# Two transformer layers on one core: the short tile moved to the front, one tile left behind the last batch, and four smaller moves

## The chip, the cores and the metric

The program runs on one core of a Trainium2 chip. The metric is the device time of one execution in microseconds, the median of the runs; lower is better. TensorE is called PE here (PEld is its weight load), VectorE DVE, ScalarE ACT, GpSimd POOL and SyncE SP.

## The reference

The input `x` has 8 batches of 100 rows of 512 values, so 800 rows. A context of 8 times 722 rows of 512 values goes beside it. Two layers follow each other, and every step is added to `x`:

```
x = x + attention0(layernorm(x), context)        # 16 heads of 32, causal
x = x + experts0(layernorm(x))                   # 8 experts, width 2048, the 2 best per row, gelu
x = x + attention1(layernorm(x), context)        # 16 heads of 64, keys and values: the
                                                 # normalised rows and a projection of the context
x = x + experts1(layernorm(x))                   # 8 experts, width 1024, the 2 best per row, silu gate
```

`experts1` ends in a norm of its own: the two answers of a row are weighted and added, the sum is normalised, multiplied by `ln_gamma`, and shifted by `ln_beta`, before it goes onto `x`. All values are float32. A layernorm needs mean and variance of each row and the reciprocal root of the variance.

## The kernel before

The 800 rows stand in SBUF as seven tiles of up to 128 partitions (`rows`, L71): six of 128 rows and a last one, tile 6, of 32. The program is written with a framework that sets all semaphores and also plans the order of the instructions on each engine: it takes what is ready by its own cost model, with the place in the program as priority, so an instruction can stand well ahead of, or behind, the place where it is written.

**Norms.** `moments` (L126) makes mean and variance on DVE (two instructions), `factors` (L134) the reciprocal root: ACT takes the root (L139, L141), DVE the reciprocal (L142) and the shift (L144). ACT holds one set of function tables at a time; the root and the exponential of the softmax are in different ones, and a load of a table shows as `ACT_TABLE_LOAD`.

**Layer 0.** After attention 0, a loop over the seven tiles (L629) projects the output, normalises it, and computes router logits one tile behind (`logits0`). When the last tile of a group is there (`GROUPS[0]`: tiles 0 to 2, 3 to 4, 5 to 6), `Route.group` (L238) picks the two best experts of each row on DVE, ranks the rows of each expert with two pairs of matmuls (L259, L260), and POOL sends each tile twice by an indirect DMA to its place in the DRAM table `sent` (L274). `Route.order` (L281) then sorts the experts by load and reads their order into registers of SP and POOL, after which SP may load the first weights of the experts.

**Experts.** `work_off` (L386) goes over eight jobs. `arrived` (L345) fetches a job's rows from `sent` and turns them on PE; `hidden0` or `hidden1` and `products` are the matmuls; `returned` (L375) writes the answers to DRAM. `midway`, where it is given, is called at the fifth job (k = 4), behind the fetch for the sixth. In layer 0 it fetches a context.

**Attention 1.** 64 units, one for each batch `b` and pair of heads `ic`, in that order. A unit computes keys and values of the context (L432, L444; 13 units read them from DRAM, where they were left earlier), the scores (L793), the softmax (L797 to L804) and, one unit later, the turned weights (`turned`, L815) and the weighted sum (`attended`, L832). The softmax's reciprocal sums must be spread over the partitions of the result. For the first three batches they are widened on POOL (L807) and turned on PE (L837). For the other batches SP writes them to DRAM and reads them back as a broadcast `over` (L810, L812), and DVE multiplies later (L850).

The seven output tiles follow as their batches end: `due` (L910 to L914) puts `output` (projection by 16 matmul passes L891, add, norm) of a tile two units behind the batch that ends it, `logits1` one unit on, and the group's routing one further. The outputs of tiles 0 to 4 come at units 18, 26, 34, 50 and 58; tiles 5 and 6 both end behind the last batch, at the end of the loop (L935). `GROUPS[1]` is (0 to 1), (2 to 3), (4), (5 to 6).

**Experts 1 and the last norm.** `gain` and `bias` are fetched on ACT's queue ahead of the jobs (L944, L946). Behind the jobs POOL gathers two answers per row and tile (`fetch`, L340), DVE weights and adds them into `acc` (L1003, L1005), normalises, multiplies by `gain`, adds to `x`, and SP writes the tile out (L1015). The add of `bias` to `x` (L1011, on POOL) is written in that last loop.

Of the kernel before, what the change touches and what calls it, by code (L numbers as in the profile page):

```python
# [13 lines left out]
P = 128  # L14
D = 512
# [22 lines left out]
ROWS = NE * NT  # L38
GROUPS = ((0, 3), (3, 5), (5, NTILE)), ((0, 2), (2, 4), (4, 5), (5, NTILE))
LAST = NT - NT // P * P  # L40

# [25 lines left out]
def two_layers(ctx: ExitStack, tc: tile.TileContext, a: dict, out: bass.AP):  # L67
    nc = tc.nc
    x_in = a["x"].rearrange("b t d -> (b t) d")
    y_out = out.rearrange("b t d -> (b t) d")  # L70
    rows = [min(P, NT - i * P) for i in range(NTILE)]  # L71

# [30 lines left out]
    x = const.tile([P, NTILE, D], F32, name="x")  # L103
    nc.vector.memset(x[:, NTILE - 1, :], 0.0)
    for i0, i1 in ((0, 1), (1, 3), (3, NTILE - 1)):
        nc.scalar.dma_start(out=x[:, i0:i1, :], in_=x_in[i0 * P : i1 * P].rearrange("(i p) d -> p i d", p=P))
    nc.scalar.dma_start(out=x[:LAST, NTILE - 1, :], in_=x_in[NT - LAST :])

# [6 lines left out]
    eps2 = const.tile([P, 1], F32, name="eps2")  # L115
    nc.vector.memset(eps2, EPS * EPS)
    rank = const.tile([P, NE], F32, name="rank")
    for e in range(NE):
# [14 lines left out]

    def factors(mv, tag, twice=False):  # L134


        r = small.tile([P, 1], F32, tag=f"r{tag}", name=f"r{tag}")
        if twice:
            nc.scalar.activation(r, mv[:, 1:], AF.Sqrt, bias=eps2, scale=1.0 + EPS)  # L139
        else:  # L140
            nc.scalar.activation(r, mv[:, 1:], AF.Sqrt, bias=eps)  # L141
        nc.vector.reciprocal(r, r)  # L142
        t = small.tile([P, 1], F32, tag=f"t{tag}", name=f"t{tag}")
        nc.vector.scalar_tensor_tensor(t, mv[:, :1], -1.0, r, ALU.mult, ALU.mult)  # L144
        return r, t
# [61 lines left out]
    class Route:  # L207


        def __init__(self, layer, psum, tag):  # L210
# [7 lines left out]
            self.sel = routes.tile([P, NTILE, NE], F32, tag="sel", name=f"sel{layer}")  # L218
            nc.vector.memset(self.sel[:, NTILE - 1, :], 0.0)
            self.before = routes.tile([P, NTILE + 1, NE], F32, tag="before", name=f"before{layer}")  # L220
# [17 lines left out]
        def group(self, i0, i1, xn, held=()):  # L238
# [6 lines left out]
            at2 = self.largest(other, self.m[1][:, i0:i1], 2)  # L245
            full = g if i1 < NTILE else g - 1
            if full:
                nc.vector.tensor_tensor(self.sel[:, i0 : i0 + full, :], at1[:, :full], at2[:, :full], ALU.add)
            if full < g:
                nc.vector.tensor_tensor(self.sel[:LAST, i1 - 1, :], at1[:LAST, full], at2[:LAST, full], ALU.add)  # L250
            for i in range(i0, i1):
# [225 lines left out]
    with tc.tile_pool(name="a0", bufs=1) as ap, tc.tile_pool(name="a0w", bufs=3) as aw, tc.tile_pool(  # L477
# [92 lines left out]
        for i in range(NTILE):  # L570
            xn = aw.tile([P, D], F32, tag="xn", name="xn0")
            scaled(xn, x[:, i, :], *factors(moments(x[:, i, :], "a0"), "a"))
            to_columns(xT, xn, i * P, rows[i], ps)
            nc.gpsimd.tensor_tensor(x[:, i, :], x[:, i, :], o_b, ALU.add)
# [46 lines left out]
        def logits0(i):  # L621
            xT = xTf[:, :, i * P : i * P + rows[i]]
            to_columns(xT, xl[:, i, :], 0, rows[i], ps)
            router_logits(route.logits, i, xT, wg0, bg0, ps, "av")
            for i0, i1 in GROUPS[0]:
                if i1 == i + 1:
                    route.group(i0, i1, lambda i: xl[:, i, :], late if i1 == NTILE else ())

        for i in range(NTILE):  # L629
            w, t0 = rows[i], i * P  # L630
            if i % 4 == 0:
# [42 lines left out]
    with f0, tc.tile_pool(name="f0w", bufs=2) as fw, tc.tile_pool(  # L674
# [57 lines left out]
        for i in range(NTILE):  # L732
# [9 lines left out]
            scaled(xn, x[:, i, :], *factors(moments(x[:, i, :], "a1"), "b", twice=True))  # L742
            to_columns(xT1, xn, i * P, rows[i], ps, gamma1, beta1)
            nc.gpsimd.tensor_tensor(x[:, i, :], x[:, i, :], bo, ALU.add)
# [4 lines left out]
    with tc.tile_pool(name="a1", bufs=1) as ap, ExitStack() as later, tc.tile_pool(  # L749
# [25 lines left out]
        def values(b, ic, mT):  # L775
# [5 lines left out]
            return mv  # L781

        def weighed(b, ic, kT, mT):

# [19 lines left out]
            nc.vector.reciprocal(sums, sums)  # L804
            if b < len(EARLY):
                over = aw.tile([T, 2, H1], F32, tag="share", name="wide1", bufs=4)
                nc.gpsimd.tensor_copy(over, sums.unsqueeze(2).to_broadcast([T, 2, H1]))  # L807
                return prs, over
# [23 lines left out]
        def attended(b, ic, v, mv, prT, over):  # L832


            po = ps.tile([P, 2, T], F32, tag="tp", name="ps_av1")
            if b < len(EARLY):
                nc.tensor.transpose(po[:, 1, :], over.rearrange("t j d -> t (j d)"), ident[:T, :T])  # L837
# [6 lines left out]
            mine = qT[:, ic, b * T : (b + 1) * T]  # L844
            if b < len(EARLY):
                wide = small.tile([P, T], F32, tag="over", name="over2")
                nc.scalar.copy(wide, po[:, 1, :])
                return nc.vector.tensor_tensor(mine, po[:, 0, :], wide, ALU.mult)
# [37 lines left out]
        def output(i):  # L886

            w, t0 = rows[i], i * P
            po = ps.tile([P, D], F32, tag="tp", name="ps_o1")
# [5 lines left out]
            xn = sends[i] = aw.tile([P, D], F32, tag="xn", name="xnf1")  # L895
            scaled(xn, x[:, i, :], *factors(moments(x[:, i, :], "f1"), "a"))

# [5 lines left out]
        def sent_on(i):  # L903

            for i0, i1 in GROUPS[1]:
                if i1 == i + 1:
                    route.group(i0, i1, lambda i: sends[i])
# [3 lines left out]
        for i in range(NTILE):  # L911
            n = min(t0 + T for t0 in range(0, NT, T) if t0 + T >= i * P + rows[i]) // T * IC + 2
            for k, step in enumerate((output, logits1, sent_on)):
# [19 lines left out]
        divide()  # L933
        attended(*before[:4], *turned(*before[4]))()
        for step, i in due[len(units)]:  # L935
# [4 lines left out]
    with tc.tile_pool(name="f1", bufs=1) as fp, tc.tile_pool(name="f1w", bufs=2) as fw, tc.tile_pool(  # L940
        name="f1p", bufs=2, space=bass.MemoryType.PSUM
    ) as ps:
        gain = fp.tile([P, D], F32, name="gain")
        nc.scalar.dma_start(out=gain, in_=a["ln_gamma"].partition_broadcast(P))  # L944
        bias = fp.tile([P, D], F32, name="bias")
        nc.scalar.dma_start(out=bias, in_=a["ln_beta"].partition_broadcast(P))  # L946
        where, more, (m1, m2) = route.where, route.more, route.m
# [27 lines left out]

        def work1(jobs, first=None):
            work_off(
                jobs, lambda e, r0, n: arrived(1, e, r0, n, fw, ps), hidden1,
                lambda e, n, h, wd: products(n, h, [wd(g) for g in range(NF // 4)], NF, fw, ps),
                lambda e, r0, n, yT: returned(1, e, r0, n, yT, fw, ps), first,  # L980
            )
# [6 lines left out]
            for e in range(NE)  # L988
        ], W_L1F)
        rest(  # L990
# [3 lines left out]

        acc = fp.tile([P, NTILE, D], F32, name="acc")
        nc.vector.memset(acc[:, NTILE - 1, :], 0.0)
        for i in range(NTILE):
# [11 lines left out]
        for i in range(NTILE):  # L1009
            w = rows[i]  # L1010
            nc.gpsimd.tensor_tensor(x[:, i, :], x[:, i, :], bias, ALU.add)  # L1011
            scaled(acc[:, i, :], acc[:, i, :], *factors(moments(acc[:, i, :], "out"), "a"))
            nc.vector.tensor_tensor(acc[:, i, :], acc[:, i, :], gain, ALU.mult)  # L1013
            nc.vector.tensor_tensor(x[:, i, :], x[:, i, :], acc[:, i, :], ALU.add)  # L1014
            nc.sync.dma_start(out=y_out[i * P : i * P + w], in_=x[:w, i, :])  # L1015

# [69 lines left out]
```

## Time and profile before

| | |
|---|---|
| median of 3 runs | 1872.75 us (1872.5 to 1874.85) |
| the profiled execution | 1873.61 us, span 1872.1 us |
| mean granted PE clock | 0.962 |
| PE busy | 1730.2 us, 92% of the span |
| DVE, ACT, POOL busy | 593.0, 482.6, 151.6 us |
| attention 0 and its outputs | to about 232 us |
| experts 0 | 247 to 636 us |
| attention 1, last unit's weights turned | 1474 us |
| first expert matmul of layer 1 | 1534.6 us |
| last expert matmul to the end | 1826 to 1872 us |

Times within the program are counted from the span's start. A profile row gives a start, a duration, the engine, the line of the kernel, the operation with its output and inputs, and in square brackets how long the engine stood idle before it and what ended that. A q behind an engine's name marks its queue of DMA issues and register work. PEclk is the share of full speed that the chip granted to PE.

### The profile page before, as it was taken

What the parts mean: (1) busy time and instruction counts of PE and PEld (TensorE: products, weight loads), DVE (VectorE), ACT (ScalarE), POOL (GpSimd) and SP (SyncE); (2) the same over time, 40 slices, a digit from 0 to 9 for tenths busy, and PEclk for the clock granted to TensorE, in tenths of its full rate; (3) what the DMA queues carried; (4) which work ended last, traced back from release to release, by engine and by line L of the source; (5) the groups of instructions that cost most, each with busy time, mean ns of one, the idle gap of its engine ahead of it and who ended that gap; (6) DMA issues with size and microseconds to landing.
All of it is one profiled execution on the core that took longest, in us unless ns stands there. A gap on an engine that the chain in (4) does not pass through costs nothing. (4 is left out here: it accounts for less than half of the span.)

```text
span 1872.1 us, 26461 instructions
## 1 busy us (share of the span) xinstructions
PE 1730.2 (92%) x10422; PEld 1308.1 (70%) x10422; DVE 593.0 (32%) x1455; ACT 482.6 (26%) x1409; POOL 151.6 (8%) x245
## 2 busy tenths in 40 slices
PE   5999899999999879999999999999999839999990
PEld 2455579999999745666666666666666528999990
DVE  4464510111111130455444333444444331111115
ACT  2364321111111131333333323333333210010110
POOL 4010310000000130000000000000000030000003
PEclk9999999999999989999999999999999969999995
DMA  9911384465555371132010300211201145555513
GB/s 367 414 64 57 119 326 167 172 224 179 205 202 217 116 269 46 32 96 72 25 48 5 60 3 4 37 6 37 26 6 15 5 179 207 200 185 204 203 72 114
DMA packets 74982, 233.35 MB, mean 125 GB/s; under 512 B 23548, under 2 KB 35952, under 8 KB 58456
## 3 DMA queue, kind: packets, MB, share of 16 engines
q1 hardware_dynamic: 53348, 183.47, 28.4%
q0 software_dynamic: 9888, 30.06, 5.0%
q10 hardware_dynamic: 11604, 17.95, 3.1%
q8 instruction: 86, 1.41, 0.3%
q14 instruction: 56, 0.46, 0.1%
HBM read 180.41 MB, written 51.05 MB: 124 GB/s over the span
## 5 line engine op out<-in xcount | busy, mean ns | idle before, releaser
L432 PE MATMUL ps_m<-cb,w 128*128 128x361 f32 x896 | 302.4, 489 | 0.0
L363 PE MATMUL ps_y<-h,w 128*128 128x256 f32 (+7 forms) x1536 | 280.5, 344 | 0.0
L363 PEld LDWEIGHTS ps_y<-h,w 128*128 128x128 f32 x1536 | 268.6, 190 | 7.9
L432 PEld LDWEIGHTS ps_m<-cb,w 128*128 128x128 f32 x896 | 172.0, 197 | 103.7 <-issue 16.9
L695 PE MATMUL ps_h<-xgT,w 128*128 128x256 f32 (+7 forms) x1024 | 188.8, 345 | 0.0
L695 PEld LDWEIGHTS ps_h<-xgT,w 128*128 128x128 f32 x1024 | 180.3, 191 | 5.7 <-ACT h L699 0.2
L799 ACT ACTIVATE pr<-ps_sc,m 100x822 f32<-100x822 f32 x128 | 119.9, 942 | 176.2 <-DVE m L797 92.9
L797 DVE TENSOR_REDUCE m<-ps_sc 100x1 f32<-100x822 f32 x128 | 123.8, 1008 | 48.4 <-PE ps_sc L793 48.4
L823 DVE COPY prT<-ps_ptA 128x500 f32<-128x500 f32 x128 | 82.0, 678 | 178.2 <-PE ps_ptA L822 178.1
L699 ACT ACTIVATE h<-ps_h,s_b 128x256 f32<-128x256 f32 (+7 forms) x128 | 56.0, 438 | 303.6 <-PE ps_h L695 303.6
L436 ACT COPY mT<-ps_m 128x361 f32<-128x361 f32 x128 | 58.8, 460 | 254.7 <-PE ps_m L432 224.9
L421 PE MATMUL ps_col<-xT,w 128*128 128x400 f32 x320 | 115.0, 517 | 1.3 <-ACT xT L168 1.3
L965 PE MATMUL ps_g<-xgT,w 128*128 128x256 f32 (+7 forms) x512 | 104.0, 347 | 0.0
L965 PE MATMUL ps_u<-xgT,w 128*128 128x256 f32 (+7 forms) x512 | 102.8, 344 | 0.0
L421 PEld LDWEIGHTS ps_col<-xT,w 128*128 128x128 f32 x320 | 61.7, 196 | 47.4 <-issue 4.3
L965 PEld LDWEIGHTS ps_g<-xgT,w 128*128 128x128 f32 x512 | 91.2, 192 | 2.9
L793 PE MATMUL ps_sc<-mT,qT 64*100 64x411 f32 (+1 forms) x512 | 92.8, 468 | 0.0
L965 PEld LDWEIGHTS ps_u<-xgT,w 128*128 128x128 f32 x512 | 90.7, 190 | 2.6
L843 PEld LDWEIGHTS ps_av<-prT,mv 128*64 128x64 f32 (+1 forms) x1536 | 67.9, 137 | 27.2 <-issue 23.9
L970 ACT ACTIVATE sg<-ps_g 128x256 f32<-128x256 f32 (+7 forms) x64 | 22.3, 348 | 238.6 <-PE ps_g L965 238.6
L843 PE MATMUL ps_av<-prT,mv 128*64 128x100 f32 (+1 forms) x1536 | 80.6, 253 | 0.0
L822 PEld LDWEIGHTS ps_ptA<-ident,pr 100*128 100x128 f32 x640 | 65.3, 141 | 21.1 <-issue 11.0
(243 smaller groups left out, 1836.1 us busy)
## 6 DMA issues: line engine op xcount, KB each, us to landing
w<-in_W SPq DMA_DIRECT2D x64, 1024.0 KB
w<-in_w_gate SPq DMA_DIRECT2D x16, 1024.0 KB
w<-in_w_up SPq DMA_DIRECT2D x16, 1024.0 KB
w<-in_w_down SPq DMA_DIRECT2D x16, 1024.0 KB
sent<-nil SPq DMA_DIRECT2D x25, 512.0 KB
answers<-nil SPq DMA_DIRECT2D x25, 512.0 KB
cb<-in_ctxT ACTq DMA_DIRECT2D x16, 722.0 KB
mT<-kept_keys SPq DMA_DIRECT2D x13, 361.0 KB
```

Source lines behind the costliest of these rows:

```text
L363: nc.tensor.matmul(py[:, k, :n], ws[f // 4][:, f % 4, dc * P : (dc + 1) * P], h[:, f, :n], start=f == 0, stop=f == nf - 1,)
L421: nc.tensor.matmul(ps[:, :HALF], w[c // 4][:, dc, (c % 4) * P : (c % 4 + 1) * P], xT[:, dc, cols], start=dc == 0, stop=dc == DC - 1,)
L432: nc.tensor.matmul(pm[:, : S // 2], w_m[ic // 4][:, dc, (ic % 4) * P : (ic % 4 + 1) * P], cb[h][:, dc, : S // 2], start=dc == 0, stop=dc = ...
L436: nc.scalar.copy(mT[:, h * (S // 2) : (h + 1) * (S // 2)], pm[:, : S // 2])
L695: nc.tensor.matmul(ph[:, :n], w[:, dc, j * P : (j + 1) * P], xg[:, dc, :n], start=dc == 0, stop=dc == DC - 1,)
L793: nc.tensor.matmul(sc[:, bank, c0:c1], qT[r, ic, q0 : q0 + T], keys_, start=True, stop=True)
L797: nc.vector.tensor_reduce(m, sc[:, :, :NKH], AX.XY, ALU.max, negate=True)
L799: nc.scalar.activation(pr.rearrange("p (a n) -> p a n", a=2), sc[:, :, :NKH], AF.Exp, bias=m, accum_out=sums[:, j : j + 1],)
L822: nc.tensor.transpose(pt[:, c, :], pr[:, T + c * P : T + (c + 1) * P], ident[:T, :T])
L823: nc.vector.tensor_copy(prT[:, : NSC - 1, :], pt)
L843: nc.tensor.matmul(po[r, 0, :], vj, prT[j][:w, c, :], start=c == 0, stop=c == NSC)
L965: nc.tensor.matmul(p_[:, :n], w_[:, dc, j * P : (j + 1) * P], xg[:, dc, :n], start=dc == 0, stop=dc == DC - 1,)
```

## The change

The 32 rows of the short tile are now rows 0 to 31, tile 0; tiles 1 to 6 have 128 rows each and start at 32, 160, 288, 416, 544 and 672 (`starts`). Everything that used `i * P` as a tile's first row uses `starts[i]`, and what treated tile 6 as short (the memset of `x`, of `sel`, of `acc`) treats tile 0 so. With these starts, `due` gives units 10, 18, 26, 42, 50 and 58 for the outputs of tiles 0 to 5, and only tile 6 comes behind the last batch. Both layers use the groups (0 to 1), (2 to 3), (4 to 5), (6).

The last unit, batch 7 and `ic` 7, spreads its reciprocal sums as the first three batches do (`turned_here`), over POOL and PE, not over DRAM. The norm of `output` in attention 1 asks for `by_power`: POOL adds the epsilon and raises the result to the power -0.5, in place of ACT's root and DVE's reciprocal. `gain` and `bias` are fetched from POOL's queue in a `midway` of the second experts; there, POOL also adds `bias` to all seven tiles of `x` and clears the first tile of `acc`.

```diff
-GROUPS = ((0, 3), (3, 5), (5, NTILE)), ((0, 2), (2, 4), (4, 5), (5, NTILE))
-LAST = NT - NT // P * P
+GROUPS = ((0, 2), (2, 4), (4, 6), (6, NTILE))
+SHORT = NT - NT // P * P
...
-    rows = [min(P, NT - i * P) for i in range(NTILE)]
+    rows = [SHORT] + [P] * (NTILE - 1)
+    starts = [0] + list(range(SHORT, NT, P))
...
-    nc.vector.memset(x[:, NTILE - 1, :], 0.0)
-    for i0, i1 in ((0, 1), (1, 3), (3, NTILE - 1)):
-        nc.scalar.dma_start(out=x[:, i0:i1, :], in_=x_in[i0 * P : i1 * P].rearrange("(i p) d -> p i d", p=P))
-    nc.scalar.dma_start(out=x[:LAST, NTILE - 1, :], in_=x_in[NT - LAST :])
+    nc.vector.memset(x[:, 0, :], 0.0)
+    nc.scalar.dma_start(out=x[:SHORT, 0, :], in_=x_in[:SHORT])
+    for i0, i1 in ((1, 2), (2, 4), (4, NTILE)):
+        of_tiles = x_in[starts[i0] : starts[i0] + (i1 - i0) * P]
+        nc.scalar.dma_start(out=x[:, i0:i1, :], in_=of_tiles.rearrange("(i p) d -> p i d", p=P))
...
+        if by_power:
+            if twice:
...
+            else:
+                nc.gpsimd.tensor_scalar(r, mv[:, 1:], EPS, None, ALU.add)
+                nc.gpsimd.tensor_tensor(r, r, half, ALU.pow)
...
+        def turned_here(b, ic):
+
+            return b < len(EARLY) or (b, ic) == (B - 1, IC - 1)
...
-            if b < len(EARLY):
+            if turned_here(b, ic):
...
-            scaled(xn, x[:, i, :], *factors(moments(x[:, i, :], "f1"), "a"))
+            scaled(xn, x[:, i, :], *factors(moments(x[:, i, :], "f1"), "a", by_power=True))
...
-            for i0, i1 in GROUPS[1]:
+            for i0, i1 in GROUPS:
...
-        attended(*before[:4], *turned(*before[4]))()
+        attended(*before[:4], *turned(*before[4]))
...
-        gain = fp.tile([P, D], F32, name="gain")
-        nc.scalar.dma_start(out=gain, in_=a["ln_gamma"].partition_broadcast(P))
-        bias = fp.tile([P, D], F32, name="bias")
-        nc.scalar.dma_start(out=bias, in_=a["ln_beta"].partition_broadcast(P))
+        gain, bias = (fp.tile([P, D], F32, name=n) for n in ("gain", "bias"))
+        acc = fp.tile([P, NTILE, D], F32, name="acc")
+
+        def fetch_gains(behind):
+
+            for t, n in ((gain, "ln_gamma"), (bias, "ln_beta")):
+                nc.gpsimd.tensor_copy(t[:1, :1], behind[:1, 0, :1])
+                nc.gpsimd.dma_start(out=t, in_=a[n].partition_broadcast(P))
+            for i in range(NTILE):
+                nc.gpsimd.tensor_tensor(x[:, i, :], x[:, i, :], bias, ALU.add)
+            nc.gpsimd.tensor_copy(acc[:1, 0, :1], behind[:1, 0, :1])
+            nc.gpsimd.memset(acc[:, 0, :], 0.0)
+
...
-        ], W_L1F)
+        ], W_L1F, fetch_gains)
...
-        acc = fp.tile([P, NTILE, D], F32, name="acc")
-        nc.vector.memset(acc[:, NTILE - 1, :], 0.0)
...
-            nc.gpsimd.tensor_tensor(x[:, i, :], x[:, i, :], bias, ALU.add)
```

## The prediction

> **What bounds the kernel now.** I read the page's busy shares first, then its forty slices, then the timeline wherever PE is not full.
>
> ```profile
> span 1872.1 us, 26461 instructions
> PE 1730.2 (92%) x10422; PEld 1308.1 (70%) x10422; DVE 593.0 (32%) x1455; ACT 482.6 (26%) x1409; POOL 151.6 (8%) x245
> PE   5999899999999879999999999999999839999990
> PEclk9999999999999989999999999999999969999995
> ```
>
> PE is the bound: 9 in nearly every slice. Time can go only where PE stands or runs slowly: at the start, around 655 to 700 us, around 1500 us, and in the tail. The digit 3 near 1500 us is the way from the last attention unit to the first expert matmul, which the timeline shows:
>
> ```profile
> 1485.36 1.13 PE L891 MATMUL ps_o<-w,qT 128*128 128x512 f32 x2 [1.41 <-DVE qT L850]
> 1493.17 8.46 PE L891 MATMUL ps_o<-w,qT 128*32 128x512 f32 x16
> 1493.27 0.17 DVE L180 COPY logits<-ps_lg 128x8 f32<-128x8 f32 x1 [3.82 <-PE ps_lg L175]
> 1505.81 8.57 POOL L1011 TENSOR_TENSOR x<-x,bias 128x512 f32<-128x512 f32 x7 [59.07 <-DMA bias<-in_ln_beta]
> 1506.26 0.15 DVE L180 COPY logits<-ps_lg 32x8 f32<-32x8 f32 x1 [1.30 <-PE ps_lg L175]
> 1508.55 0.98 DVE L235 TENSOR_TENSOR at<-at,first 128x16 f32<-128x16 f32 x1
> 1514.51 0.17 DVE L235 TENSOR_TENSOR at<-at,first 128x16 f32<-128x16 f32 x1
> 1521.21 0.86 POOL L274 DMA_INDIRECT sent<-xnf,where  x1 [0.31 <-issue]
> 1527.75 1.19 POOL L351 DMA_DIRECT2D xg<-sent  x2 [5.67 <-issue]
> 1534.59 3.08 PE L965 MATMUL ps_g<-xgT,w 128*128 128x256 f32 x8
> ```
>
> The two outputs behind the last batch run one after the other: tile 5's logits are there at 1493.27, then 8.46 us of projection for 32 rows, a second norm, and logits at 1506.26. The planner has pulled the bias adds (L1011) forward to 1505.81, onto the routing: the same DVE operation takes 0.98 us beside them and 0.17 after. Inside the attention, at the third of its five output tiles:
>
> ```profile
> 1127.79 5.03 PE L432 MATMUL ps_m<-cb,w 128*128 128x361 f32 x16
> 1137.50 1.28 ACT L799 ACT_TABLE_LOAD   x1 [3.01 <-issue]
> 1139.89 0.41 PE L793 MATMUL ps_sc<-kT,qT 64*100 64x100 f32 x2 [1.55 <-ACT pr L799]
> 1140.82 0.47 PE L793 MATMUL ps_sc<-kT,qT 64*100 64x100 f32 x2 [0.51 <-ACT pr L799]
> 1141.43 1.88 PE L175 MATMUL ps_lg<-p_w_router,xTf 128*128 128x8 f32 x8
> 1143.16 7.43 PE L432 MATMUL ps_m<-cb,w 128*128 128x361 f32 x16
> 1141.00:1148.00 7.00, 6.85 (x19) 0.51 0.07 3
> ```
>
> The root left its table in ACT, so the next exponential first loads its own (1.28 us), PE waits 1.55 and 0.51 us for the exponentials, and then (last line, from the windows: start and end, length, PE busy, granted clock, DMA) the clock is 0.51 and the same sixteen matmuls take 7.43 us, not 5.03. All five tiles show it, the first with a wait of 1.33 alone.
>
> **The end of attention 1, part by part** (times against the profiled span).
>
> *Last unit's sums over PE.* SP loses three DMA issues. PE's 1.41 us wait goes. Added are a POOL copy (rows: 0.29), a PE transpose (0.30) and an ACT copy (0.24); sums are ready at 1475.6 and PE waits 0.76 us for the turned weights at 1477, so they hide. Without that cover 0.3 more. **-1.4.**
>
> *One tile behind the batch.* From 1493.27 to 1506.26 there is only tile 6's own chain. It leaves: **-13.0.** What comes late next is the routing itself, at once behind the first logits.
>
> *Routing of one tile, without the adds beside it.* From logits (1506.26) to the last `before` (1515.29) it takes 9.03 us. The group of tile 4 alone ran the same steps undisturbed from 1431.81 to 1434.57, 2.76 us. **-6.2.**
>
> *Two sends, not four.* POOL issues a send each 1.27 us, so the last starts 2.43 us sooner. More: the first weights, bound to the expert order and not to the sends, start at 1522; the fourth send's rows move only at 1525.5, behind the first megabyte, and the fetch waits 5.67 us. Two sends would be through by 1521. But the fetch's 512 KB then meets two megabytes of weights (1522 to 1528.5, 286 to 337 GB/s): served early it lands near 1525.5, served last near 1530.1, against 1531.1 now. Bounds -1.0 and -5.6; I take **-2.8**, nearer the late end as the fourth send itself was held for a whole megabyte.
>
> *Power for root.* Out go ACT's root (0.29), a reciprocal (0.16) and their handover, 0.56 us from statistics to L144. In come two POOL instructions on 128x1. No row shows a power. Below: a 1x1 copy on POOL is 0.12, so -0.2 in all; above: two adds of 128x512 at 1.26, so +2.0. One element per partition is nearest to the small rows: **+0.4.** Behind POOL's wait for the statistics stand the next widening copy and later sends, none due within a unit.
>
> Sum of the end: **-23.0.**
>
> **Inside attention 1.** Tile 0's output now runs at unit 10, where PE is full: sixteen passes 7.13 (row at 1120.82), transposes 0.43 and logits 0.42 as for the 32 rows now, with their overlap **+7.6**. No exponential needs a reload: five times 1.28, **-6.4**; a sixth tile brings the rest of the wait (0.27 + 0.51, less early on), **+0.6**. The slow clock: sixteen L432 passes took 8.05, 7.43, 6.80 and 6.57 us against 5.03, eight took 5.14 against 2.70, which is 11.1; the logits passes, against 0.95 in layer 0, 2.7 more, so 13.8 in all. Whether the clock still falls with 0.78 us of waiting is open: bounds 0 and -13.8. A lone wait of 0.63 us at 807 left it full, so I take two thirds, **-9.0**. Sum **-7.2**.
>
> The Trainium skill speaks against this term. Its page "TensorE: Matmul & The Clock Gate" (section "Part 1: The HAM clock gate") has the clock halve after at least one idle window of about 3.4 us; no wait here is that long, so by it the reloads would not be the cause and removing them would return none of the nine: about 1853.4 us in all. The trace has the clock at half within 3.5 us of each of five waits of 1.3 to 2.1 us, so the sum goes by the rows.
>
> **The rest.** Layer 0's groups: POOL's last send starts at 231.28 and its fetch lets PE wait 2.33 us at 244.44. Now group (4, 5) comes just ahead of group (6), so six sends follow tile 5's logits instead of four, 2.5 us more, but the DVE and PE no longer route in the middle of tile 5 and 6 (a PE wait of 1.05 at 214.99) and start sooner: **0**, bounds ±2. Ahead of attention 1 the full tile is last: its gather carries 128 rows, its four ACT copies 0.48 each instead of 0.38: **+0.5**, bounds ±2 as the planner's order there changes. At the start the first load of `x` waits for the 0.48 us memset; PE stands for its weights until 18.78 anyway; a larger last transpose **+0.3**. In the tail the last tile writes 256 KB instead of 64, at 197 GB/s 1.0 us more, less 0.3 for the short first gather: **+0.7**.
>
> *Midway.* POOL stands idle from 1683.8 to 1706.8. Into these 23 us go the wait for the fetched rows (about 4), two copies and two issues (1.3), the landing (about 5), seven adds (8.8) and the memset (0.6): 19.7. Behind them wait job 4's answers, not read before 1835, and a fetch due one job ahead. DVE's products L971 (0.34 to 0.42) may stretch to the 1.2 us that L232 reached beside the adds; 2.0 us of idle before each covers it; uncovered, some at a job's end would cost up to 3. **+0.3.** ACT's two issues at 1501.7 go free.
>
> Rest: **+1.8**. Together -23.0 - 7.2 + 1.8 = **-28.4** on a span of 1872.1. The profiled execution took 1873.61, 0.86 over the median; set against the median, 1872.75 - 28.4 = **1844.4 us**.
>
> **The rivals.**
>
> *The clock keeps falling* behind each output tile, as the logits passes load weights more than they compute. For: the shortest wait (1.33, at 924.53) had as long a dip as any. Against: none at 807. Then +9.0, about 1853.
>
> *The interior keeps its waits*, because the planner puts the scores elsewhere or PE waits for the exponential itself. Against: ACT's load row is 1.28 of the 1.55. Then +6.4 and +9.0: 1860.
>
> *The midway adds do not land midway.* L1011 and the memset show how far the planner moves them. They can't precede the sixth fetch, but could stand in front of the gathers: 8.8 us, 1853.
>
> *More than forecast:* no dip at all (-4.8), the fetch served early (-2.8), layer 0 shorter (-1): 1836.
>
> *Slower:* the power is slow. Price p for the pair, once in full at the end; inside, scaled rows are ready at 1007.2 and turned at 1013.96, so six tiles each stall p - 7.2. Saving and loss meet at 7p = 28.8 + 0.45 + 43.2, p = 10.3 us, eight times the 128x512 add. Little speaks for it.
>
> **How the numbers follow.** Forecast 0.50, falling clock 0.20, interior waits 0.08, adds in the tail 0.06, more 0.10, slow power or another loss as large 0.05, no change 0.01. A measurement can tell 0.2%, 3.7 us, from nothing. Faster 0.93, same 0.02 (half of it from the edge of the interior rival), slower 0.05. The range holds all but the slow power and the outer halves of two rivals: from 1835 (no dips, early fetch) to 1860 (dips and waits stay).
>
> **What would show it.** After: logits of tile 6 near 1486 and one group behind them with 0.17 us operations; the first L965 some 30 us earlier than 1534.6; no `ACT_TABLE_LOAD` between output tiles; L432 at 5.0 us behind the logits; L1011's successor on POOL near 1660 to 1675. Wrong it would be made by a POOL power over a microsecond, by slow-clock windows that stay, or by new gaps near 235 or 670 us.

## The result and the profile after

The changed kernel takes 1852.7 us (median; 1850.7 to 1854.6), beside 1873.8 us of the kernel before in the same set of runs (1872.5 to 1878.5): a ratio of 0.9882, 95% interval 0.9865 to 0.9900. The forecast was 1844.4 us, 8.3 us less; the time lies within the stated 1835 to 1860. The profiled execution took 1852.47 us. Its page, the lines that answer to those of before:

```profile
span 1851.0 us, 26473 instructions
PE 1725.6 (93%) x10427; PEld 1305.7 (71%) x10427; DVE 583.7 (32%) x1467; ACT 465.5 (25%) x1390; POOL 159.5 (9%) x266
PE   4999899999999969999999999999999959999990
PEclk9999899999999979999999999999999979999995
```

PE is busy 4.6 us less, in a span 21.1 us shorter: what went is mostly standing time. The 3 in PE's row near 1500 us is a 5 now. The timeline of the changed kernel from the last tile's norm to the first expert matmul, and the shift midway:

```profile
1489.21 0.57 POOL L148 TENSOR_TENSOR ra<-ra,half 128x1 f32<-128x1 f32 x1
1489.81 0.16 DVE L156 SCALAR_TENSOR_TENSOR ta<-mv_f,ra 128x1 f32<-128x1 f32 x1 [1.00 <-POOL ra L148]
...
1494.37 0.17 DVE L192 COPY logits<-ps_lg 128x8 f32<-128x8 f32 x1 [3.81 <-PE ps_lg L187]
1494.77 0.17 DVE L243 TENSOR_TENSOR at<-logits,m 128x8 f32<-128x8 f32 x1
1497.00 0.12 DVE L263 TENSOR_TENSOR before<-before,sel 128x8 f32<-128x8 f32 x1
1500.80 0.98 POOL L285 DMA_INDIRECT sent<-xnf,where  x1 [0.30 <-DVE most L327]
1506.59 1.19 POOL L362 DMA_DIRECT2D xg<-sent  x2 [4.82 <-DMA w<-in_w_gate]
1513.77 2.17 PE L989 MATMUL ps_g<-xgT,w 128*128 128x256 f32 x8
...
1635.06 8.63 POOL L967 TENSOR_TENSOR x<-x,bias 128x512 f32<-128x512 f32 x7 [2.59 <-DMA bias<-in_ln_beta]
```

One set of logits, at 1494.37; DVE's routing runs at 0.17 us an instruction and is through at 1497.12, 2.75 us later, against 9.03 before. The adds of `bias` lie at 1635, beside the experts. Inside the attention, the third output tile's logits in the same timeline:

```profile
1023.96 0.41 PE L808 MATMUL ps_sc<-kT,qT 64*100 64x100 f32 x2 [0.27 <-ACT pr L814]
1024.89 0.41 PE L808 MATMUL ps_sc<-kT,qT 64*100 64x100 f32 x2 [0.51 <-ACT pr L814]
1025.51 1.24 PE L187 MATMUL ps_lg<-p_w_router,xTf 128*128 128x8 f32 x8 [0.20 <-ACT xTf L173]
1026.60 6.62 PE L443 MATMUL ps_m<-cb,w 128*128 128x361 f32 x16
```

There is no `ACT_TABLE_LOAD` between the tiles any more, and the wait of 1.55 us is one of 0.27. But the sixteen L443 passes take 6.62 us and not the 5.03 they need at full clock: by the trace's clock record PE stood at half clock from 1026.2 for 3.4 us. That happens at four of the first six tiles, 13.7 us at half clock in all; before, it was 27.3 us at five tiles.

Where the time went, in four stretches of the two profiled executions (the second ends where PE starts to turn the last unit's weights):

| stretch | before | after | change | forecast |
|---|---|---|---|---|
| start to the first scores of attention 1 | 759.3 | 763.7 | +4.4 | +0.8 |
| to the last unit's turned weights | 714.8 | 710.8 | -4.0 | -7.2 |
| to the first expert matmul of layer 1 | 60.5 | 39.3 | -21.2 | -23.0 |
| to the end of the span | 337.5 | 337.2 | -0.3 | +1.0 |

These are single executions: in two more of the changed kernel (e5 and e12) the four stretches take 764.5, 710.8, 37.1 and 339.6 us, and 763.2, 710.8, 39.6 and 339.0.

### The profile page after: what moved, and what is told of

Its sections match the earlier page's. It is cut to its first block, busy times and chain, and to the rows that moved or that the text cites. A ratio compares the mean times of both kernels' runs of the same rounds, so it can differ in the third digit from the quotient of the medians.

```text
span 1851.0 us, 26473 instructions
## 1 busy us (share of the span) xinstructions
PE 1725.6 (93%) x10427; PEld 1305.7 (71%) x10427; DVE 583.7 (32%) x1467; ACT 465.5 (25%) x1390; POOL 159.5 (9%) x266
## 4 chain that ended last, share of the span: by engine, by line
PE 65%; issue 20%; DMA 10%; DVE 3%; ACT 1%; POOL 0%; POOLq 0%; ACTq 0%; another core or an unknown queue 0%; DVEq 0%
PE ps_m L443 17%; PE ps_col L432 7%; DMA answers<-y 6%; PE ps_sc L808 5%; PE ps_g L989 4%; PE ps_u L989 4%; PE ps_av L858 4%; PE ps_y L374 4%; PE ps_v L890 3%; PE ps_ptA L837 3%; PE ps_o L906 3%; PE ps_mv L455 2%; PE ps_v L535 2%; DMA back<-answers,where 1%; PE ps_o L646 1%
## 5 line engine op out<-in xcount | busy, mean ns | idle before, releaser
L443 PE MATMUL ps_m<-cb,w 128*128 128x361 f32 x896 | 297.3, 482 | 0.0
L443 PEld LDWEIGHTS ps_m<-cb,w 128*128 128x128 f32 x896 | 169.4, 194 | 102.1 <-issue 14.0
L706 PE MATMUL ps_h<-xgT,w 128*128 128x256 f32 (+7 forms) x1024 | 187.5, 344 | 0.0
L706 PEld LDWEIGHTS ps_h<-xgT,w 128*128 128x128 f32 x1024 | 179.2, 190 | 5.3 <-ACT h L710 0.2
L838 DVE COPY prT<-ps_ptA 128x500 f32<-128x500 f32 x128 | 82.1, 678 | 168.5 <-PE ps_ptA L837 168.5
L808 PE MATMUL ps_sc<-mT,qT 64*100 64x311 f32 (+1 forms) x512 | 93.1, 468 | 0.0
```

What stands on the lines that cost most here:

```text
L443: nc.tensor.matmul(pm[:, : S // 2], w_m[ic // 4][:, dc, (ic % 4) * P : (ic % 4 + 1) * P], cb[h][:, dc, : S // 2], start=dc == 0, stop=dc = ...
L706: nc.tensor.matmul(ph[:, :n], w[:, dc, j * P : (j + 1) * P], xg[:, dc, :n], start=dc == 0, stop=dc == DC - 1,)
L808: nc.tensor.matmul(sc[:, bank, c0:c1], qT[r, ic, q0 : q0 + T], keys_, start=True, stop=True)
L838: nc.vector.tensor_copy(prT[:, : NSC - 1, :], pt)
```

## The experiments

Three sets of four kernels, on three chips. The median of the kernel before was 1871.2, 1874.5 and 1876.1 us in them, that of the changed kernel 1853.4 and 1853.6 in the second and third; executions of one kernel differ by 3 to 10 us. The first set (e1 to e4) has no run of the changed kernel beside it, and there the kernel before was 3.3 to 4.9 us faster than in the others: set against it, e1 to e4 stand 3 to 5 us worse than their medians say; which comparison is right isn't known. So a few microseconds are read from the stretches of the traces, and the medians stand beside them. "Inside" is the second stretch of the table (710.8, 710.8 and 710.8 us in three executions of the changed kernel), "end" the third (39.3, 37.1, 39.6).

| run | median us (lowest to highest) | ratio to the kernel before |
|---|---|---|
| e1 root on ACT and DVE | 1867.3 (1863.3 to 1873.1) | 0.9981 (0.9970 to 0.9992) |
| e2 adds early | 1857.2 (1855.2 to 1860.1) | 0.9916 (0.9900 to 0.9932) |
| e3 last unit over DRAM | 1853.8 (1852.7 to 1855.8) | 0.9904 (0.9889 to 0.9920) |
| e4 layer 0's groups as before | 1853.8 (1851.3 to 1856.5) | 0.9906 (0.9890 to 0.9923) |
| e5 the changed kernel | 1853.4 (1849.9 to 1855.4) | 0.9877 (0.9858 to 0.9897) |
| e6 tiles and groups as before | 1854.3 (1851.4 to 1859.2) | 0.9888 (0.9867 to 0.9909) |
| e7 short tile last in layer 0 | 1852.2 (1850.0 to 1857.1) | 0.9883 (0.9861 to 0.9904) |
| e8 weights behind the rows | 1855.0 (1853.4 to 1857.5) | 0.9890 (0.9872 to 0.9909) |
| e9 logits one unit later | 1850.5 (1847.2 to 1852.7) | 0.9864 (0.9845 to 0.9883) |
| e10 short tile last, but first in the gathers | 1850.2 (1848.5 to 1853.0) | 0.9864 (0.9847 to 0.9881) |
| e11 e9 and e10 together | 1845.9 (1843.9 to 1847.3) | 0.9839 (0.9825 to 0.9853) |
| e12 the changed kernel | 1853.6 (1850.5 to 1854.4) | 0.9875 (0.9859 to 0.9892) |

### e1: the root back on ACT

```diff
-            scaled(xn, x[:, i, :], *factors(moments(x[:, i, :], "f1"), "a", by_power=True))
+            scaled(xn, x[:, i, :], *factors(moments(x[:, i, :], "f1"), "a"))
```

> The changed kernel, with the root of the output norms of attention 1 taken by ACT and DVE again, as before. Theory of the prediction (the table reload makes PE wait, and the wait halves the clock): six tiles are followed by exponentials, so six loads of 1.28 us come back, the waits at the logits grow from 0.51 to about 1.55 us, and the stretches of half clock behind them go from 3.4 to 6.8 us at most tiles, 1.7 us each: 7.7 + 5 to 10 - 0.4 for the power at the end, so 12 to 17 us slower than the changed kernel, about 1867. Rival (the stretches of half clock come from the narrow logits passes and not from the reload): the waits alone come back, 6 to 8 us slower, and every stretch stays at 3.4 us. Rival (the reload is hidden): within 1 us.

The median is 13.8 us over the changed kernel's in the other two sets. The timeline of e1 at the third tile:

```profile
1027.42 1.28 ACT L814 ACT_TABLE_LOAD   x1 [3.01 <-issue]
1029.81 0.41 PE L808 MATMUL ps_sc<-kT,qT 64*100 64x100 f32 x2 [1.55 <-ACT pr L814]
1030.74 0.55 PE L808 MATMUL ps_sc<-kT,qT 64*100 64x100 f32 x2 [0.51 <-ACT pr L814]
1031.36 1.88 PE L187 MATMUL ps_lg<-p_w_router,xTf 128*128 128x8 f32 x8
1033.08 7.39 PE L443 MATMUL ps_m<-cb,w 128*128 128x361 f32 x16
```

and its windows behind that (start and end, length, busy time of PE, weight loads, DVE, ACT and POOL, granted clock, DMA share, GB/s):

```profile
1031.00:1038.00 7.00, 6.93 (x19) 4.71 (x19) 0.28 (x2) 0.30 (x1) 0.00 (x0) 0.52 0.02 0
```

With the load come the wait of 1.55 us and a half clock of 6.8 us. Inside takes 725.0 us, 14.2 more. Six loads of 1.28 are 7.7; the half clock sums to 27.3 us and not 13.7, and half of the difference is 6.8: 14.5. Both parts of the theory are there; the rival that leaves the clock out falls short by half. (The other stretches of this one profile sum to 1.9 us less than in the changed kernel's first.)

### e2: the adds as early as before

```diff
-        def fetch_gains(behind):
...
+        bias = fp.tile([P, D], F32, name="bias")
+        nc.scalar.dma_start(out=bias, in_=a["ln_beta"].partition_broadcast(P))
...
         for i in range(NTILE):
             w = rows[i]
+            nc.gpsimd.tensor_tensor(x[:, i, :], x[:, i, :], bias, ALU.add)
```

> The changed kernel, with gain and bias fetched ahead of the experts and the adds of bias where they were written before. In POOL's order the seven adds now stand behind the power of tile 6 and ahead of its two sends, from about 1490 to 1498.5. Theory of the prediction (the adds stretch the routing on DVE, 0.17 us to about 1 us an instruction): the routing from 1494.4 on runs at a fifth of its speed until 1498.5, so some 3.3 us are lost, 3 to 4.5 us slower. Rival (the routing took 9 us before only because it was one of two tiles): the DVE instructions stay at 0.17 us, and only the sends, which are issued behind the adds, could be late: 0 to 0.5 us.

The timeline of the routing in this kernel:

```profile
1491.43 8.58 POOL L1026 TENSOR_TENSOR x<-x,bias 128x512 f32<-128x512 f32 x7 [1.24 <-DMA bias<-in_ln_beta]
1494.92 0.16 DVE L241 TENSOR_REDUCE m<-logits 128x1 f32<-128x8 f32 x1
1495.12 1.25 DVE L243 TENSOR_TENSOR at<-logits,m 128x8 f32<-128x8 f32 x1
1498.85 1.18 DVE L256 SCALAR_TENSOR_TENSOR other<-at,logits 128x8 f32<-128x8 f32 x1
1500.26 0.17 DVE L243 TENSOR_TENSOR at<-other,m 128x8 f32<-128x8 f32 x1
1501.30 0.13 DVE L263 TENSOR_TENSOR before<-before,sel 128x8 f32<-128x8 f32 x1
```

Until POOL is through at 1500.01, each DVE instruction with two operands waits for about one add (0.99 to 1.25 us), and each reduction takes 0.16 as ever; the same L243 takes 1.25 beside the adds and 0.17 behind them. From logits to `before` it is 6.7 us against 2.75, the end takes 43.7 against 39.3, and the median is 3.8 us above those of the other two sets: the theory's 3 to 4.5.

### e3: the last unit over DRAM

```diff
-            return b < len(EARLY) or (b, ic) == (B - 1, IC - 1)
+            return b < len(EARLY)
```

> The changed kernel, with the last unit's reciprocal sums spread over DRAM again. Theory of the prediction: a wait of 1.41 us in front of the last output comes back, 1.4 us slower. Rival from the trace of the changed kernel (between the last turned weights and the logits it takes 19.9 us and not 18.1, with a stretch of half clock from 1476.8 that the kernel before has not): the sums over PE bought that stretch, so the time stays within 0.7 us or gets up to 1 us shorter, and the stretch is gone.

PE's wait is back, and in this execution no half clock begins near 1476 (its timeline):

```profile
1484.41 1.12 PE L906 MATMUL ps_o<-w,qT 128*128 128x512 f32 x2 [1.52 <-DVE qT L865]
```

The end takes 39.3 us. The eight executions of kernels that share the changed kernel's end fall into two kinds: with a half clock that begins between 1473 and 1477 (39.3, 39.6, 39.6, 39.6) and without (36.9, 37.1, 37.5, 37.8). So over PE the sums gain 1.4 to 2.4 us where the clock stays full, and nothing where it falls; the one wait ahead of it is 0.86 us for the last exponential, in both kinds, in e3 and in the kernel before. The rival's time, within 0.7 us, fits the four with the fall. That the sums bring the fall, as it has it, isn't shown: four executions have the sums and a full clock, and only two, e3 and the kernel before, are without the sums.

### e4: layer 0's groups as before

```diff
-GROUPS = ((0, 2), (2, 4), (4, 6), (6, NTILE))
+GROUPS = ((0, 3), (3, 5), (5, NTILE)), ((0, 2), (2, 4), (4, 6), (6, NTILE))
```

> The changed kernel, with layer 0's groups as before: tiles 0 to 2, 3 to 4, 5 to 6. Theory from the trace of the changed kernel (the group of tiles 4 and 5 is routed in the middle of tile 6: PE waits 1.34 and 1.44 us there and then runs at half clock for 13.7 us instead of 6.8): the first matmul of experts 0 comes 2 to 4 us sooner, and half to all of it stays to the end, 1 to 4 us faster. Rival (the 5 us that are lost by then come from the full tile at the end and from the start, whatever the groups): no change, within 0.7 us, with the first matmul of experts 0 still near 252.

From the first output projection of layer 0 to the first matmul of experts 0 it takes 87.3 us; in the changed kernel 85.5, 85.7 and 85.6, before 82.4. The groups are not where the time was lost: the theory falls. In e4, as in the changed kernel, the last tile of layer 0 has 128 rows.

### e5 and e12: the changed kernel again

> The changed kernel itself, beside the three others, for their comparison and for how its trace differs from execution to execution: 1850 to 1856 us. If the 1.8 us of the start come from the order of the loads, the first projection of queries starts at 36 to 37 us again; if they are scatter, anywhere from 34 to 37.

> The changed kernel once more, to stand beside these three on the same chip: 1850 to 1856 us. The places of the half-clock stretches in attention 1 show how far they move from execution to execution: four or five of them, 13 to 17 us in all.

Medians 1853.4 and 1853.6. Inside is 710.8 us in all three profiles, with 13.7 us of half clock each time, though e5 has it in two stretches of 6.8 us and the others in four of 3.4. In e2 and e10, which leave the attention as it is, it is 712.5 and 712.7 us: there the clock fell once more, behind the 32-row tile 0, after one wait of 0.27 us. The first projection of queries starts anywhere from 33.9 to 36.6 us in the nine executions of kernels that take the short tile first (mean 35.4), and from 33.9 to 34.9 in the five that take it last (mean 34.4): 1 us between the means, less than the scatter among the nine.

### e6: tiles and groups as before, with the other three parts

```diff
-GROUPS = ((0, 2), (2, 4), (4, 6), (6, NTILE))
-SHORT = NT - NT // P * P
+GROUPS = ((0, 3), (3, 5), (5, NTILE)), ((0, 2), (2, 4), (4, 5), (5, NTILE))
+LAST = NT - NT // P * P
...
-    rows = [SHORT] + [P] * (NTILE - 1)
-    starts = [0] + list(range(SHORT, NT, P))
+    rows = [min(P, NT - i * P) for i in range(NTILE)]
```

> The kernel before with three of the four parts: the power in the output norms, the last unit's sums over PE, and the shift midway; tiles and groups stay as before, so two tiles still follow the last batch. By the prediction's terms the tiles and groups are worth -13.0 and -2.8 behind the batch, +7.6 and +0.6 inside the attention, +1.5 elsewhere: -6.1, so this kernel lies 6 us over the changed one, about 1859. With the 3 us that layer 0's end was seen to lose it is 3 us over, about 1856. Rival (one tile behind the batch is what shortened the routing from 9.0 to 2.8 us too, and the adds only lay beside it): 12 us over, about 1865.

The timeline of its end, two tiles in the last group and no adds beside it:

```profile
1497.36 0.15 DVE L186 COPY logits<-ps_lg 32x8 f32<-32x8 f32 x1 [1.35 <-PE ps_lg L181]
1500.29 0.16 DVE L258 TENSOR_TENSOR before<-before,sel 128x8 f32<-128x8 f32 x1
1506.58 0.87 POOL L280 DMA_INDIRECT sent<-xnf,where  x1 [0.30 <-issue]
1513.24 1.21 POOL L357 DMA_DIRECT2D xg<-sent  x2 [5.80 <-issue]
1519.80 2.44 PE L984 MATMUL ps_g<-xgT,w 128*128 128x256 f32 x6
```

The routing of two tiles takes 3.09 us from logits to `before`, so it was the adds, not the second tile, that made 9.03 of it: the rival falls. The end takes 54.1 us, 14.4 to 16.9 more than in the changed kernel. Inside takes 704.9, 5.9 less, and the stretch ahead of it 760.9, 2.8 less than in the changed kernel's first profile. The medians differ by 0.9 us, less than the two intervals can tell; by the profiled executions it is 5 to 7 (this kernel's was the slowest of its five). So the short tile's move, the largest term of the forecast at one place, is worth 1 to 7 us in all, and the power, the shift midway and the last unit's sums make the rest of some 21, 14 to 20.

### e7 and e10: the short tile last in layer 0

```diff
-            for i0, i1 in GROUPS:
-                if i1 == i + 1:
+            for i0, i1 in GROUPS0:
+                if i1 == p + 1:
...
-        for i in range(NTILE):
+        for p, i in enumerate(TURNS):
...
+GROUPS0 = ((0, 3), (3, 5), (5, NTILE))
+TURNS = [*range(1, NTILE), 0]
```

> The changed kernel, but layer 0 takes its tiles in the order 1 to 6, 0 (load, norm, outputs, groups of three, two and two, and the gathers behind the experts), so that the short tile is the last one there, as before; attention 1 and its groups are as in the changed kernel. Theory (layer 0's end lost 3 us because the last tile's transposes, logits passes and sends carry 128 rows and not 32): the first matmul of experts 0 follows the first output projection by 82.5 us again and not by 85.5, so 2 to 4 us faster. Rival (the loss comes from the half clock there, whatever the rows): it stays at 85 and the time within 0.7 us.

The last send of layer 0, the first fetch and the first expert matmul, in the changed kernel's timeline and then in that of e7:

```profile
234.28 0.96 POOL L285 DMA_INDIRECT sent<-xl,where  x1 [0.30 <-issue]
244.05 1.18 POOL L362 DMA_DIRECT2D xg<-sent  x2 [8.80 <-PE ps_mv L455]
252.45 1.89 PE L706 MATMUL ps_h<-xgT,w 128*128 128x256 f32 x8
```

```profile
231.66 0.87 POOL L294 DMA_INDIRECT sent<-xl,where  x1 [0.30 <-issue]
239.28 1.19 POOL L373 DMA_DIRECT2D xg<-sent  x2 [6.75 <-PE ps_mv L466]
247.40 2.97 PE L718 MATMUL ps_h<-xgT,w 128*128 128x256 f32 x13
```

From the first output projection it is 82.1 us to that matmul, as before the change. From the last send's issue to the fetch it takes 7.6 us here, 7.4 before, and 9.8 in the changed kernel: with 128 rows in each of the last two sends, four times as much must land, beside the first weights. (The releaser that the fetch's row names, PE, was at work all along and is not what the fetch needs.) But behind the experts as much is lost: from their last hidden matmul (L706, here L718) to the first scores 152.6 us, against 146.9 to 149.8 in the nine executions that take the short tile first as the changed kernel does. In e7's waits of PE there:

```profile
649.90 1.11 PE L466 MATMUL ps_mv<-ident,mT 128*128 128x128 f32 x4 [5.03 <-ACT mT L458]
657.56 0.66 PE L466 MATMUL ps_mv<-ident,mT 128*128 128x128 f32 x4 [1.76 <-ACT mT L458]
665.94 0.73 PE L466 MATMUL ps_mv<-ident,mT 128*128 128x128 f32 x4 [2.64 <-ACT mT L458]
```

The changed kernel has 3.97, 0.45 and 2.35 us in their place. ACT's copies of `mT` stand behind the roots of the gathered tiles' norms, and these behind DVE's sums and POOL's gathers. e10 keeps the order of layer 0 and lets the gathers begin with the short tile (the cut is against e7):

```diff
-        for p, i in enumerate(TURNS):
-            w = rows[i]
+        for i in range(NTILE):
+            w, p = rows[i], TURNS.index(i)
             both = fp.tile([P, 2, D], F32, tag="nil", name="back0", bufs=2)
```

> The changed kernel with the short tile last in layer 0's norms, outputs and routing, and first again in the gathers behind the experts. In the run with the short tile last in the gathers too, 3.4 us were gained ahead of experts 0 and as many lost behind them, where PE waited 9.4 us in all for ACT's copies of mT and not 6.3 to 6.7. Theory (the chain of gather, sum, statistics and root, which stands ahead of those copies on ACT, is short where the first gathered tile is): the gain stays, 3 to 4 us faster than the changed kernel. Rival (the wait behind the experts depends on when the gathers start, whatever tile is first): within 1 us.

Now it is 83.4 us ahead of the experts and 147.3 behind them; the median is 3.4 us under the changed kernel's (the ranges overlap; the two stretches give about 4). e11, with the same layer 0, has 82.0 and 149.1. So the gain ahead of the experts stays, as the theory has it; that the chain of gathers and roots is the reason is read from the traces and not tested by itself. One thing stays open: the kernel before, with the short tile last at both places, took 148.4 us there in its one profile, while e6 and e7 took 152.5 and 152.6.

### e8: the first weights behind the rows

```diff
-        route.order(lambda: weights.load(W_L1F + 2))
+        route.order(lambda: None)
```

> The changed kernel, but in layer 1 the first two weight pieces too are loaded only behind the first fetched rows, as the next six are; layer 0 is untouched. It tests the reading that the sends of tile 6, and so the fetch at 1506.6, are held by the two megabytes of weights that start at 1501.5. Theory: the sends land by 1503.5, the fetch starts near 1503.5 and lands near 1508, the first weight tile lands 3 to 4 us behind that, the first expert matmul comes at 1511 to 1513 and not at 1513.8: 0 to 3 us faster, as a gain at the fetch that the later weights eat in part. Rival (the fetch waits for the sends' own time, whatever else moves): the fetch stays near 1506, and the weights come 4 to 6 us late: 4 to 6 us slower.

The timeline of its end, from the last send:

```profile
1498.60 0.98 POOL L285 DMA_INDIRECT sent<-xnf,where  x1 [0.31 <-DVE most L327]
1502.47 1.19 POOL L362 DMA_DIRECT2D xg<-sent  x2 [2.88 <-DMA sent<-xnf,where]
1513.47 2.90 PE L989 MATMUL ps_g<-xgT,w 128*128 128x256 f32 x6 [3.48 <-DMA w<-in_w_gate]
```

From the last send's issue to the fetch 3.9 us, against 5.8: the weights did hold the sends, as the theory has it. But then PE waits 3.48 us for the weights; the end takes 41.2 us, 1.6 to 4.1 more, and the median is 1.6 up, where the theory had 0 to 3 us less. Holding the weights back until the rows are fetched gains nothing. That it need not be one or the other shows in e1's one profile: the first weights are issued 0.8 us behind the start of the last send there (0.7 in the changed kernel's three), the fetch still comes 4.0 us behind that send, and the end takes 36.2 us, less than in any other run (the root on ACT makes 0.4 of the difference).

### e9 and e11: the logits passes one unit later

```diff
+        def columns1(i):
+            turned1[i] = qT[:, :DC, starts[i] : starts[i] + rows[i]]
+            to_columns(turned1[i], sends[i], 0, rows[i], ps)
...
         def sent_on(i):
+            logits1(i)
...
-            for k, step in enumerate((output, logits1, sent_on)):
+            for k, step in enumerate((output, columns1, sent_on)):
```

> The changed kernel, but in attention 1 the logits passes of a tile are written one unit behind its transposes (the turned rows lie until then in columns of qT that are already used). In PE's order of the changed kernel the next unit's first scores stand between a tile's transposes and its logits passes, ahead of that unit's L443 passes, and wait 0.27 and 0.51 us for exponentials; here they come behind the L443 passes as in any other unit. Theory (the waits, few as they are, halve the clock): the waits go, 0.8 to 1 us at five tiles, and with them the four stretches of 3.4 us at half clock, 1.7 us each: 9 to 12 us faster than the changed kernel, about 1843. Rival (the stretches come from the logits passes, eight matmuls of 8 columns with a weight load each): the waits go but the stretches stay: 3 to 5 us faster. Rival (the waits turn up at the next scores): within 1 us.

The timeline of PE at the third tile, which ends no group, and at the fourth, which does:

```profile
1031.71 1.06 PE L187 MATMUL ps_lg<-p_w_router,qT 128*128 128x8 f32 x8
1032.62 5.11 PE L443 MATMUL ps_m<-cb,w 128*128 128x361 f32 x16
...
1235.71 1.06 PE L187 MATMUL ps_lg<-p_w_router,qT 128*128 128x8 f32 x8
1237.57 0.54 PE L808 MATMUL ps_sc<-kT,qT 64*100 64x100 f32 x2 [0.45 <-ACT pr L814]
1239.79 0.61 PE L270 MATMUL ps_rank<-before,every 128*128 128x16 f32 x2 [1.68 <-DVE before L263]
1240.66 7.03 PE L443 MATMUL ps_m<-cb,w 128*128 128x361 f32 x16
```

The windows behind the two, with the granted clock third from the end:

```profile
1032.00:1038.00 6.00, 6.00 (x28) 4.11 (x29) 0.98 (x4) 2.34 (x7) 0.00 (x0) 1.00 0.06 6
1237.00:1245.00 8.00, 5.87 (x16) 3.78 (x15) 3.66 (x23) 0.65 (x3) 2.45 (x3) 0.57 0.14 41
```

The same logits passes, without a wait ahead of them, leave the clock at 1.00; so it does at all three tiles that end no group, here and in e11. At the three that do, the routing now follows the logits at once, PE's rank matmuls wait 1.51 to 1.81 us for DVE, and there the clock falls. So the logits passes do not halve the clock by themselves. But a wait is not needed for it either. The timeline of PE in e4, behind the transposes of tile 1:

```profile
935.98 0.41 PE L808 MATMUL ps_sc<-kT,qT 64*100 64x100 f32 x2
936.90 0.41 PE L808 MATMUL ps_sc<-kT,qT 64*100 64x100 f32 x2
937.78 1.06 PE L187 MATMUL ps_lg<-p_w_router,xTf 128*128 128x8 f32 x8
938.69 4.37 PE L443 MATMUL ps_m<-cb,w 128*128 128x361 f32 x8
```

No row waits here, and yet the clock record has 3.4 us at half from 939.1, and the eight L443 passes take 4.37 us (2.68 in the changed kernel, same rows, full clock). Of the ten executions that have this passage without a wait, the clock fell in two (here and in e6). Behind the waits of 0.27 and 0.51 us it fell at 36 of the 40 tiles in the same ten. So waits go with the half clock, and where they are longer it is longer (e1); that they alone make it isn't shown. e9 also puts a whole unit between a tile's transposes and its logits passes, and how much of its full clock is due to that, no run tells apart. In the time the theory was wrong, 3.1 us and not 9 to 12, since this edit put new waits in: the half clock sums to 17.1 us, and inside takes 709.7 us, 1.1 less. The ranges of the two medians overlap, and of the gain in the profiles 2.6 us lie ahead of attention 1, which the edit leaves alone. The groups' routing one unit later still was not run.

> The two runs above in one kernel. If each keeps what it gains, their sum: 6 to 16 us faster than the changed kernel, 1838 to 1848. If the gain in layer 0 is given back again, as the first of them alone.

The two together: 1845.9 us, 7.7 under the changed kernel beside it, and the two ranges of times do not overlap. This is the fastest version of the study, 0.9839 (0.9825 to 0.9853) of the kernel before. In the profiles 5.1 us of the gain lie ahead of attention 1, 0.4 inside it, and 2.7 in the end, where the clock stayed full at the last unit: most of it is layer 0's order and the place of the waits in the clock's grid, and little is e9's edit.

## Why the prediction was right, and where it was off

It had the sign and nearly all of the main term: of the 23.0 us at the end, 21.2 came in the first profile and 23.3 in e5's. It missed 7.3 us of 28.4 between the two profiled executions: 3.6 ahead of attention 1, 3.2 inside it, 1.8 at the end, less 1.3 won behind it. That 1852.7 lies beside the 1853 of two of the rivals (the clock that keeps falling, the adds in the tail) is chance: three quarters of the clock's term came, the adds did land midway, and the miss is the sum of several small ones.

- *One tile behind the batch, -13.0, and two sends, -2.8.* e6 undoes both: 14.4 to 16.9 us for 15.8. Held. The reason for the sends, that the weights hold them, is borne out by e8 (5.8 us became 3.9).
- *Routing of one tile without the adds, -6.2.* Held: 9.03 became 2.75. e6 and e2 show that the adds did it, 3.1 us for two tiles without them and 6.7 for one with them.
- *Last unit's sums over PE, -1.4.* Held where the clock stays full, nothing where it falls. The cover that was named, 0.76 us at 1477, is idle time of the weight loads; PE itself computes output passes there (its row at 1476.12 runs to 1477.24). The term left the clock out.
- *Power for root, +0.4.* From statistics to the factor 1.00 us, against 0.56: 0.44. Held; the rival of a slow power is out, with 0.23 and 0.57 us for the pair.
- *Five table reloads, -6.4.* Held: from before to e6, inside goes from 714.8 to 704.9, by 10.0, where the reloads are 6.4 and the half clock, 27.3 to 20.5 us, is 3.4: 9.8.
- *The slow clock, -9.0.* The term that was mis-sized: in the changed kernel half of (27.3 - 13.7), -6.8. "A lone wait of 0.63 us at 807 left it full, so I take two thirds" failed: behind the 0.27 and 0.51 us that stayed the clock comes down at most tiles, for 3.4 us more often than 6.8. The rival "the clock keeps falling" had 2.2 of its 9.0 us. The Trainium skill's rule, weighed against the term (no loss of clock without an idle window of 3.4 us), is not what the traces show: with no wait above 1.55 us, e1's reloads take the half clock from 13.7 to 27.3 us.
- *Tile 0's output, +7.6, and a sixth wait, +0.6.* From e6 to the changed kernel inside grows by 5.9 while the half clock falls from 20.5 to 13.7 us: 9.3 without the clock. Short by 1.1.
- *Layer 0's groups, 0.* The step that failed: "the DVE and PE no longer route in the middle of tile 5 and 6 ... and start sooner". The group (4, 5) is now routed in the middle of tile 6 (PE waits 1.34 and 1.44 us there), but e4 shows that this isn't the price either. The price, 3.1 to 3.6 us, is that of the 128 rows of the last tile, of which the prediction counted the sends and not their size; with the short tile last again, e7 gets 3.5 and e10 2.2 of it back.
- *Full tile last ahead of attention 1, +0.5.* 148.4 to 149.1 us in these two profiles, but 146.9 to 149.8 over nine executions with this order: too small to tell. e6 and e7, with the short tile last in the gathers, took 152.5 and 152.6, and why the kernel before was at 148.4 is open.
- *Start, +0.3.* +2.0 to the first projection of queries in these two profiles; 1 between the means of fourteen executions, less than their scatter.
- *Midway, +0.3, and tail, +0.7.* The last stretch is 0.3 us shorter in the first profile, 2.1 and 1.4 longer in e5 and e12: the 1.0 lies within the scatter. The adds came one job earlier than forecast (1635, not 1660 to 1675), and the products that were to stretch did not: L995 takes 0.39 us beside them and behind them.

## What to carry to other kernels

When a wait is to go, ask what stays of it: here the clock fell behind 0.78 us as it did behind 2.06, mostly for half as long, and now and then where PE did not wait at all. A shorter wait made the half clock shorter and did not rule it out. When a small tile changes its place, price it at every place where it was last or first, in rows and bytes and not in instructions: some 16 us were won behind the last batch, and 6 lost inside the attention and 3 at the end of layer 0. And what lies idle on one engine may not be free for another: seven adds that nobody waited for cost 4 to 6 us because they ran beside a chain of two-operand instructions on DVE.

## What the runs showed of the hardware

**The half clock comes in steps of 3.41 us on a fixed grid.** In each of the fourteen traces the stretches start whole multiples of 3.413 us apart (in the changed kernel 2, 56, 183, 190, 292, 353, 382, 411, 424, 428 and 521 steps behind the first). Where the waits lie in that grid changes from execution to execution: e5 and e12 run the same program with the same waits, one with two stretches of 6.8 us, the other with four of 3.4. At the last unit the clock came down behind the same 0.86 us in four of the eight executions of e3's comparison, and in two of ten without any wait (the rows of e4 under e9). What the chip counts as idle the runs do not show. The Trainium skill, "TensorE: Matmul & The Clock Gate", section "Part 1: The HAM clock gate", says that the window of 3413 ns runs freely and does not start with the kernel; the traces agree. Its condition for the fall, at least one idle window, they do not show: in the changed kernel's attention the waits ahead of a fall add up to between 0.78 and 0.98 us, under a third of one.

**A DVE instruction with two operands in SBUF waits for POOL's, one with a single operand or an operand in PSUM does not.** Beside 128x512 adds on POOL (about 1.23 us each), two-operand instructions of 128x8 took 0.99 to 1.25 us, reductions 0.16, and products with one operand in PSUM 0.39 as without. POOL's adds took 8.58 us beside the routing and 8.63 midway. The Trainium skill, "SBUF — State Buffer", section "Who interferes with whom", says the same of DVE instructions with two inputs in SBUF; the runs agree.
